# Layer 0 of a conv/attention hybrid: each tile's norm factor and turned y at once, x's last convolution in two blocks, weight products between layer 1's sums

## The chip, the cores and the metric

The kernel runs on one core of a Trainium2 chip. A core has five engines that work side by side and meet at semaphores: PE (TensorE, matrix products into PSUM; its weight loads are listed as PEld), DVE (VectorE), ACT (ScalarE, functions of one input from a table), POOL (GpSimd, which does not read PSUM here) and SP, which starts transfers. Each engine runs its instructions in the order in which they were written to its queue. The metric is the device time of one execution in microseconds (us), as the median of several runs.

## The reference

The input x has 4 images of 256 channels and 32 x 32 pixels (1024 tokens an image, 4096 in all). Four layers follow one another; the change lies in layer 0 and layer 1. Cut to what matters:

```python
# layer 0: a state-space block (Mamba 2), then channel attention
u = layernorm(x as tokens)
z, xBC, dt = split(u @ in_w.T)                 # 256, 256 + 128 + 128, 4 heads
xBC = silu(causal_conv4(xBC) + conv_b)         # per channel, 4 taps along the tokens
x_s, Bm, Cm = split(xBC)
y = scan(dt, A, x_s, Bm, Cm) + Dp * x_s        # recurrence along the tokens of an image
y = y * silu(z)
y = y * rsqrt(mean(y * y, -1) + 1e-5) * rms_w  # norm factor of each token
out = y @ out_w.T
pooled = mean(out, over the image's tokens)
attn = sigmoid(relu(pooled @ se1_w.T + se1_b) @ se2_w.T + se2_b)
x = x + out * attn                             # attn: one number per image and channel
# layer 1: non-local block with one inner channel, batch norm over everything
g, theta, phi = 1x1 convolutions of x to one channel
y = theta * sum(phi * g) / N                   # per image
x = x + batch_norm(w_w * y)                    # needs sums over all 4096 tokens
# layer 2: self-attention, q = u Wq + bq, k = u Wk + bk, then a mixture of experts
# layer 3: another attention, then an LSTM of 1024 steps
```

## The kernel before

All of x stays in SBUF as `rows`, 32 tiles of 128 tokens by 256 channels. In layer 0 an image is `b` (`B` = 4) and a tile within it `c` (`TPI` = 8). `W` is 512 tokens, `BPI` = 2 such blocks an image, `C` = 2 groups of 128 channels.

**`_project`** (L236 on) goes over eight blocks of 512 tokens: transpose, norm, transpose back, and the product with `in_w`. `z` goes through Silu into `zs`; `xBC` lands transposed (channels on partitions) in `xbc[b]`, four groups m of 128 channels: 0 and 1 are x, 2 is B, 3 is C. Three columns of zeros stand ahead of the tokens (`off` = `DCONV` - 1), for the taps. After each second block the finished image is convolved (`convolve`): `_convolution` multiplies one tap on ACT and adds three on DVE (L340), all 1024 tokens at once, and Silu writes the result over the raw values. The last image is not convolved there: `_convolve_last` does it group by group beside the scan of image 0, with Tanh in place of Silu, so that ACT keeps the table that it needs for the scan (silu(a) = a/2 (1 + tanh(a/2)); the taps are halved for that). At the end of the projection `_decays` makes the exponentials of dt for all tiles, which every scan tile needs.

**`_scan`** (L403) does one tile: PE turns x and B (`ptr`), ACT copies them (`xb`), POOL makes `xdt`, `y` and `xw` from them, PE, ACT and DVE make the decay matrix `m_h`, PE the products `py` and `pst`, DVE adds up y and carries the `state` to the next tile. At last DVE multiplies `zs` by y, and ACT squares it and sums the square of each token into a column of `ss` (L462).

**`_attention`** (L492) is run for a whole image once its eight tiles are scanned, for images 0 to 2 after the second tile of the next image (L219), for image 3 at the end. POOL turns eight columns of `ss` into the norm factor `rstd` (L506, and L507 with a power of -0.5). DVE scales the identity by it, once a tile (`diag`, L514). PE multiplies `zs` by that diagonal, which turns y and norms it in one product (L518); ACT copies 512 tokens at a time over the x groups of `xbc`, which the scan needs no more, and sums them on the way (`part`, L522). `pooled` (L527) goes through the two small attention products, and the result scales the output weights (`w_att`). `_out` (L567) multiplies each turned tile by `w_att` and adds to `rows`. For images 0 to 2 these products stand beside the next image's scan; four of image 2 and all of image 3 stand at the end.

**`_query_weights`** (L580) makes Wq Wk^T (`m_qk`) and bq Wk (`b_qk`) for layer 2, at the end of layer 0. **`_layer1`** (L601) has three sums over partitions, each a product with a matrix of ones (`dots`, `sum`, `sum2`), with short DVE and POOL steps between, then a row (`p_row`, L661) that everything after it adds to `rows`.

What sets the order: a planner. The program issues instructions with their tiles; the planner lists them per engine, those written earlier first where several could run, by its own durations, and adds the semaphores. `issue_after(ins)` holds instructions of PE behind another one in the same queue. PSUM has eight banks: in the scan two each for `ptr`, `pst` and `p_o` (turns, attention and `_out`), one each for `pd` and `py`. Each queue then runs strictly in that order.

Of the kernel before, what the change touches and what calls it, by code (L numbers as in the profile page):

```python
# [169 lines left out]
def _layer0_and_1(s):  # L170
# [5 lines left out]
    with ExitStack() as ctx:  # L176
# [22 lines left out]
            dtr=keep.tile([P, NT, NH], F32, name="dtr"),  # L199
            ss=keep.tile([P, NT], F32, name="ss"),  # L200
        )
        for x in v.xbc:
            nc.gpsimd.memset(x[:, :, :off], 0.0)
        with tc.tile_pool(name="conv", bufs=2, side="right") as conv, ExitStack() as body:
# [10 lines left out]
            for b in range(B):  # L215
                for c in range(TPI):
                    _scan(s, v, pools, b, c)
                    if b == 0 and c % 2 == 0:
                        _convolve_last(s, v, pools, conv, c // 2)  # L219
                    if b == 0 and c == TPI - 1:  # L220
                        _out_weights(s, v, pools)
                    if b > 0 and c == 1:
                        held = _attention(s, v, pools, b - 1)
                    if b > 0 and c >= TPI // 2:
                        n = 1 if b == B - 1 else 2
                        for j in range(n * (c - TPI // 2), n * (c - TPI // 2 + 1)):
                            _out(s, v, pools, b - 1, j, held, "p_o")
# [4 lines left out]
            for j in range(TPI):  # L232
                _out(s, v, pools, B - 1, j, last, "ptr")
            _query_weights(s, pools.ps)
        _layer1(s, v)


def _project(s, v, keep, conv):
# [4 lines left out]
    with ExitStack() as ctx:  # L243
# [65 lines left out]
        def convolve(b):  # L309
            for m in range(NXBC):  # L310
                acc = _convolution(s, v, conv, b, m, s.col["conv_w"], s.col["conv_b"])
                nc.scalar.activation(v.xbc[b][:, m, off:], acc, AF.Silu)
# [4 lines left out]
        for i in range(NBLK):  # L317
            if i + 2 < NBLK:
                load(i + 2)
            if i + 1 < NBLK:  # L320
                turn(i + 1)
            project(i)
            if i == NBLK - 1:
                v.decays = _decays(s, keep, pool, ps, v.dtr)
            if i % BPI == BPI - 1 and i + 1 < NBLK:
                convolve(i // BPI)


def _convolution(s, v, conv, b, m, w, bias):

    nc = s.nc
    off = DCONV - 1
    x = v.xbc[b][:, m, :]
    acc = conv.tile([P, L], F32, name="acc")
    tap = w[:, m * DCONV : (m + 1) * DCONV]
    nc.scalar.activation(
        acc, x[:, off:], AF.Identity, bias=bias[:, m : m + 1], scale=tap[:, off:]
    )
    for j in range(off):
        nc.vector.scalar_tensor_tensor(  # L340
            acc, x[:, j : j + L], tap[:, j : j + 1], acc, ALU.mult, ALU.add
        )
    return acc


def _convolve_last(s, v, pools, conv, m):
# [3 lines left out]
    if m == 0:  # L350
# [3 lines left out]
        nc.gpsimd.tensor_scalar_mul(v.half_b, s.col["conv_b"], 0.5)  # L354
    acc = _convolution(s, v, conv, B - 1, m, v.half_w, v.half_b)
    dst = v.xbc[B - 1][:, m, DCONV - 1 :]
    nc.scalar.activation(dst, acc, AF.Tanh)
# [45 lines left out]
def _scan(s, v, pools, b, c):  # L403
# [3 lines left out]
    (a, head), xbc, zs = v.decay, v.xbc[b], v.zs[b]  # L407
    off = DCONV - 1
    if c == 0:
        v.state = pool.tile([P, NH, HD], F32, name="state")  # L410
    state = v.state
    n = b * TPI + c
    t = slice(off + c * P, off + (c + 1) * P)
    bT, cT = xbc[:, 2, t], xbc[:, 3, t]

    ptr = ps.tile([P, 4, P], F32, name="ptr")
    for m in range(3):
        nc.tensor.transpose(ptr[:, m, :], xbc[:, m, t], s.ident)
    nc.tensor.matmul(ptr[:, 3, :], bT, cT, start=True, stop=True)
# [68 lines left out]


def _attention(s, v, pools, b, beside=()):  # L490


# [11 lines left out]

    rstd = pool.tile([P, TPI], F32, name="rstd")
    nc.gpsimd.tensor_scalar(rstd, v.ss[:, bass.ts(b, TPI)], 1.0 / D, EPS, ALU.mult, ALU.add)  # L506
    nc.gpsimd.tensor_tensor(rstd, rstd, s.power, ALU.pow)  # L507
    yT = v.xbc[b][:, :C, DCONV - 1 :]
    part = pool.tile([P, C, BPI], F32, name="part")
    for i in range(BPI):  # L510
        diag = pool.tile([P, TPB, P], F32, name="diag")
        for j in range(TPB):
            n = i * TPB + j
            nc.vector.tensor_scalar_mul(diag[:, j, :], s.ident, rstd[:, n : n + 1])  # L514
        for k in range(C):
            p = small(P, W)
            for j in range(TPB):
                nc.tensor.matmul(  # L518
                    p[:, bass.ts(j, P)], v.zs[b][:, i * TPB + j, bass.ts(k, P)], diag[:, j, :],
                    start=True, stop=True,  # L520
                )
            nc.scalar.activation(  # L522
                yT[:, k, bass.ts(i, W)], p, AF.Identity, accum_out=part[:, k, i : i + 1]
            )

    pooled = pool.tile([P, C], F32, name="pooled")
    nc.vector.tensor_reduce(pooled, part, AX.X, ALU.add)  # L527
    p = small(NSE, 1)
# [35 lines left out]
    nc.scalar.copy(w[:, :, D:], p.rearrange("p (m i) -> p m i", i=3))  # L564
    return yT, w


def _out(s, v, pools, b, j, held, tag):

    nc = s.nc  # L570
    yT, w = held
    n = b * TPI + j
    p = pools.ps.tile([P, W], F32, name="p_y", tag=tag)[:, : D + 3]
    for k in range(C):
        nc.tensor.matmul(p, yT[:, k, bass.ts(j, P)], w[:, k, :], start=k == 0, stop=k == C - 1)
    nc.vector.tensor_add(s.rows[:, n, :], s.rows[:, n, :], p[:, :D])
# [3 lines left out]
def _query_weights(s, ps):  # L580

    nc = s.nc
    wq, wk = (s.w_l2[:, :, j * D : (j + 1) * D] for j in range(2))
    s.m_qk = s.const.tile([P, C, D], F32, name="m_qk")
    s.b_qk = s.const.tile([P, C], F32, name="b_qk")
    for m in range(C):
        p = ps.tile([P, W], F32, name="p_q", tag="p_o")
        for k in range(C):
            nc.tensor.matmul(
                p[:, :D], wq[:, k, bass.ts(m, P)], wk[:, k, :], start=k == 0, stop=k == C - 1  # L590
            )
        nc.scalar.copy(s.m_qk[:, m, :], p[:, :D])
        for k in range(C):
            nc.tensor.matmul(
                p[:, D : D + 1], wk[:, k, bass.ts(m, P)], s.col["bq"][:, k : k + 1],
                start=k == 0, stop=k == C - 1,
            )
        nc.vector.tensor_copy(s.b_qk[:, m : m + 1], p[:, D : D + 1])


def _layer1(s, v):  # L601
# [4 lines left out]
    with ExitStack() as ctx:  # L606
# [3 lines left out]
        def new(name, *shape):  # L610
            return pool.tile([P, *shape], F32, name=name)

        w2, wg = new("w2", C), new("wg", C)
# [14 lines left out]
        dots = ps.tile([P, B], F32, name="dots")  # L628
        nc.tensor.matmul(dots, s.ones, dot, start=True, stop=True)
        y = s.l1_y = s.const.tile([P, NT], F32, name="l1_y")  # L630
# [6 lines left out]
        def total(name, values):  # L637

            p = ps.tile([P, 1], F32, name=name)
            nc.tensor.matmul(p, s.ones, values, start=True, stop=True)  # L640
            mean = new(f"{name}_mean", 1)
# [16 lines left out]
        for k in range(C):  # L658
            diag = new(f"diag{k}", P)
            nc.vector.tensor_scalar_mul(diag, s.ident, scale[:, k : k + 1])  # L660
            nc.tensor.matmul(p[:, bass.ts(k, P)], s.ones, diag, start=True, stop=True)  # L661
        s.l1_row = s.const.tile([P, D], F32, name="l1_row")
# [1309 lines left out]
```

## Time and profile before

| what | us |
|---|---|
| median of 3 runs (lowest, highest) | 3417.93 (3415.67, 3419.51) |
| the profiled execution, device time | 3415.7 |
| its span, first to last instruction | 3413.9 |
| projection, from the start | about 130 |
| scans of images 0, 1, 2, 3 end (last `zs` product) | 185.0, 223.3, 268.9, 310.8 |
| `pooled` of image 3 | 321.8 |
| last `_out` added to `rows` | 336.2 |
| row of layer 1 ready | 345.2 |

A line of the timeline has the start in us, the length in us, the engine, the line of the kernel, the instruction, its output and inputs with their shapes, and how many it stands for; in square brackets the idle time of that engine before it and what ended it. A line of the groups has the busy time, the mean in ns of one, and the idle time before them. The windows give busy time by engine between two points of time. The granted clock is PE's, 1.00 being full. Most matrix products of fp32 are two instructions each.

### The profile page before, as it was taken

The page shows a single profiled execution, that of the slowest core. Times are in us where ns is not written, and L with a number is a line of the kernel's source. Part 1 is how long each engine was busy: PE and PEld are TensorE (multiplying, and loading weights), DVE is VectorE, ACT ScalarE, POOL GpSimd, SP SyncE. Part 2 cuts the span into 40 slices and gives each one's busy share as a digit, 9 for nine tenths or more (in the row PEclk, how much of TensorE's full clock was granted, in tenths as well). Part 3 has the DMA queues.
Part 4 walks back from the last instruction along what each step waited for, and adds up shares of the span by engine and source line. Part 5 has one row for each costly group of instructions (what it writes and reads, how often), then busy time and mean ns, then how long its engine had stood idle before and what let it go on. Part 6 is the DMA issues. An engine that isn't in the chain of part 4 may idle for free.

```text
span 3413.9 us, 143838 instructions
## 1 busy us (share of the span) xinstructions
PE 3103.3 (91%) x63668; PEld 2493.0 (73%) x63668; DVE 1836.3 (54%) x8185; ACT 1093.6 (32%) x4351; POOL 535.0 (16%) x751
## 2 busy tenths in 40 slices
PE   8888899999999989998988988998998998998887
PEld 5476577688888857777777777777777777777776
DVE  6775654651111144565655555565655555655555
ACT  6754222222222222332332332332332332332222
POOL 2342100124444320001001001001001001001000
PEclk9999899999999999999999999999999999999999
DMA  2000011356666620000000000000000000000000
GB/s 78 10 1 1 1 38 38 109 169 197 194 194 216 193 61 2 4 4 10 4 4 10 4 4 10 4 4 10 4 4 10 4 4 10 4 4 8 6 4 10
DMA packets 49221, 140.28 MB, mean 41 GB/s; under 512 B 4944, under 2 KB 38032, under 8 KB 43856
## 3 DMA queue, kind: packets, MB, share of 16 engines
q0 software_dynamic: 18768, 101.03, 9.6%
q1 hardware_dynamic: 27680, 24.45, 2.2%
q8 instruction: 500, 8.19, 1.0%
q10 hardware_dynamic: 2144, 5.55, 0.5%
q14 instruction: 129, 1.06, 0.1%
HBM read 105.78 MB, written 25.22 MB: 38 GB/s over the span
## 4 chain that ended last, share of the span: by engine, by line
PE 42%; DVE 21%; ACT 11%; issue 5%; ACTq 0%; DMA 0%; POOL 0%; DVEq 0%; SPq 0%; POOLq 0%
PE pre L1797 16%; DVE col L1808 11%; PE ph L1292 7%; PE po L1301 7%; PE pre L1741 6%; ACT tri L1811 5%; DVE scan L1820 5%; DVE hs L1831 4%; PE p_a L1695 3%; PE p_d L1397 1%; PE p_k L1365 1%; PE p_x L1266 0%; ACTq L1811 0%; PE p_w L856 0%; DMA acc<-y,late_rows 0%
## 5 line engine op out<-in xcount | busy, mean ns | idle before, releaser
L1797 PE MATMUL pre<-w_v,hs 128*4 128x64 f32 x49104 | 873.5, 219 | 208.0 <-DVE hs L1831 197.3
L1797 PEld LDWEIGHTS pre<-w_v,hs 128*4 128x4 f32 x49104 | 684.8, 86 | 396.6 <-DVE hs L1831 393.6
L1741 PE MATMUL pre<-xg,pick 128*128 128x64 f32 x6144 | 903.3, 283 | 0.6 <-DVE xg L1708 0.6
L1741 PEld LDWEIGHTS pre<-xg,pick 128*128 128x128 f32 x6144 | 762.9, 191 | 118.2 <-DVE xg L1708 0.9
L1808 DVE STREAM_TRANSPOSE col<-pre 128x64 f32<-128x64 f32 x2048 | 484.5, 250 | 303.9 <-PE pre L1797 289.3
L1811 ACT ACTIVATE tri<-col 128x16 f32<-128x16 f32 x1024 | 229.5, 224 | 1175.4 <-DVE col L1808 1175.4
L1820 DVE TENSOR_TENSOR_SCAN scan<-tri 128x24 f32<-128x24 f32 x1024 | 216.2, 211 | 360.7 <-ACT tri L1811 360.7
L1703 POOL TENSOR_TENSOR xg<-xg,gate_bias 128x192 f32<-128x192 f32 x127 | 74.9, 590 | 1597.9 <-ACT xg L1702 1597.9
L1292 PE MATMUL ph<-xT,wt 128*128 128x256 f32 (+1 forms) x1184 | 253.8, 370 | 2.2 <-ACT hT L1295 1.3
L1295 ACT ACTIVATE hT<-ph,wt 128x256 f32<-128x256 f32 (+1 forms) x296 | 136.6, 462 | 353.1 <-PE ph L1292 343.8
L1301 PE MATMUL po<-wt,hT 128*128 128x256 f32 x1120 | 249.1, 379 | 0.0
L1292 PEld LDWEIGHTS ph<-xT,wt 128*128 128x128 f32 x1184 | 205.7, 189 | 42.8 <-ACT hT L1295 7.4
L1301 PEld LDWEIGHTS po<-wt,hT 128*128 128x128 f32 x1120 | 209.8, 190 | 27.0
L1829 DVE STREAM_TRANSPOSE gate<-row 128x64 f32<-128x64 f32 x1024 | 228.1, 223 | 1.0
L1818 ACT ACTIVATE row<-pre 128x64 f32<-128x64 f32 x1024 | 210.2, 205 | 0.9
L1836 DVE SCALAR_TENSOR_TENSOR tri<-hs,scan 128x8 f32<-128x8 f32 x1023 | 181.5, 177 | 36.1 <-DVE hs L1831 1.5
L1270 DVE COPY xT<-p_x 128x512 f32<-128x512 f32 (+1 forms) x37 | 24.5, 662 | 205.1 <-PE p_x L1266 205.0
L1312 DVE TENSOR_TENSOR y<-po,wt 128x256 f32<-128x256 f32 x70 | 29.6, 424 | 185.8 <-PE po L1301 185.8
L1695 PE MATMUL p_a<-w_u,u 128*32 128x192 f32 x1792 | 119.3, 338 | 0.0
L822 PE MATMUL p_s<-u,q 128*128 128x512 f32 x256 | 117.0, 597 | 0.0
L856 PE MATMUL p_w<-v,prT 128*128 128x256 f32 x512 | 116.0, 379 | 0.7 <-ACT prT L848 0.7
L856 PEld LDWEIGHTS p_w<-v,prT 128*128 128x128 f32 x512 | 95.5, 190 | 15.5 <-issue 2.9
(2474 smaller groups left out, 3277.3 us busy)
## 6 DMA issues: line engine op xcount, KB each, us to landing
xn<-xn SPq DMA_DIRECT2D x8, 516.0 KB, 3.5
x<-in_x_dram SPq DMA_DIRECT2D x16, 256.0 KB, 3.2
acc<-rows SPq DMA_DIRECT2D x8, 512.0 KB, 2.9
out_dram<-part SPq DMA_DIRECT2D x64, 64.0 KB, 1.7
xn_early<-xn SPq DMA_DIRECT2D x6, 516.0 KB, 5.1
rows<-acc SPq DMA_DIRECT2D x6, 512.0 KB, 8.6
w_l<-in_w_l_dram ACTq DMA_DIRECT2D x1, 1092.0 KB, 9.6
rows<-acc SPq DMA_DIRECT2D x4, 256.0 KB, 4.5
```

The costliest lines, as they stand in the source:

```text
L856: nc.tensor.matmul(p, prT[:, n, :], images[g // TPI].v[:, n, :], start=n == 0, stop=n == TPI - 1)
L1292: nc.tensor.matmul(ph, w1[:, k, bass.ts(m, P)], xT[:, k, :], start=k == 0, stop=k == C - 1)
L1301: nc.tensor.matmul(po, hT[:, m, bass.ts(j, P)], w2[:, m, :], start=m == 0, stop=m == NHC - 1)
L1695: nc.tensor.matmul(p[32 * j : 32 * (j + 1), :], u3[i * SG // P][:, k, bass.ts(i % (P // SG), 32)], w_u[:, k, j * Q : (j + 1) * Q], start=k ...
L1741: nc.tensor.matmul(p, pick[:, r].rearrange("p j r -> p (j r)"), xg[i][:, v], start=True, stop=t == 0,)
L1797: nc.tensor.matmul(p[32 * j : 32 * j + B, :], hs[:, t - 1, k * B : (k + 1) * B], w_v[:, k, j * Q + v.start : j * Q + v.stop], start=False, ...
L1808: nc.vector.transpose(col[:, g * C : (g + 1) * C, :].rearrange("p n r -> p (n r)"), pre[t % 2][g])
L1811: nc.scalar.activation(z[:, 2:50].rearrange("p (g q) -> p g q", g=2)[:, :, ::3].rearrange("p g (k b) -> p (g k) b", k=C), col[:, :, :B], A ...
L1818: nc.scalar.activation(row, pre[t % 2][2], AF.Tanh)
L1820: nc.vector.tensor_tensor_scan(scan, z[:, 0 : 3 * S], z[:, 26 : 26 + 3 * S], 0.0, ALU.mult, ALU.add)
L1829: nc.vector.transpose(gate.rearrange("p n r -> p (n r)"), row)
L1836: nc.vector.scalar_tensor_tensor(tri[(t + 1) % 2][:, 28:52:3], h, 0.5, cell, ALU.mult, ALU.mult)
```

## The change

Four things are done differently.

1. The norm factor, the diagonal, the turn and the copy of y are made for each tile right behind its scan (`_by_channel`), not for the image. The factor is made in place in the tile's column of `ss`. Each tile's copy is two ACT instructions of 128 columns, whose sums go into `part`, now one column a tile.
2. The x groups (m = 0, 1) of the last image are convolved in two blocks of 512 tokens: the first in `_project` behind block 6, with Silu, its result written from column 0 on (three columns ahead of its old place, so that the raw values that the second block's taps need stay); the second beside image 0's scan as before. `_tokens` gives the columns of a tile's tokens.
3. `_query_weights` is handed out in pieces: the first matrix behind the first sum of layer 1, the second behind the third, the biases behind the products of the row; each has PSUM banks of its own.
4. `_attention` begins at `pooled`.

```diff
             for b in range(B):
                 for c in range(TPI):
                     _scan(s, v, pools, b, c)
+                    _by_channel(s, v, pools, b, c)
...
                 _out(s, v, pools, B - 1, j, last, "ptr")
-            _query_weights(s, pools.ps)
         _layer1(s, v)
...
             if i % BPI == BPI - 1 and i + 1 < NBLK:
                 convolve(i // BPI)
+            if i == NBLK - BPI:
+                for m in range(C):
+                    acc = _convolution(
+                        s, v, conv, B - 1, m, slice(0, W), s.col["conv_w"], s.col["conv_b"]
+                    )
+                    nc.scalar.activation(v.xbc[B - 1][:, m, :W], acc, AF.Silu)
+
+def _tokens(b, lo, hi):
+    off = 0 if b == B - 1 and hi <= W else DCONV - 1
+    return slice(off + lo, off + hi)
...
-    acc = _convolution(s, v, conv, B - 1, m, v.half_w, v.half_b)
-    dst = v.xbc[B - 1][:, m, DCONV - 1 :]
+    lo = W if m < C else 0
+    acc = _convolution(s, v, conv, B - 1, m, slice(lo, L), v.half_w, v.half_b)
+    dst = v.xbc[B - 1][:, m, DCONV - 1 + lo :]
...
+def _by_channel(s, v, pools, b, c):
+    nc, pool = s.nc, pools.out
+    n = b * TPI + c
+    rstd = v.ss[:, n : n + 1]
+    nc.gpsimd.tensor_scalar(rstd, rstd, 1.0 / D, EPS, ALU.mult, ALU.add)
+    nc.gpsimd.tensor_tensor(rstd, rstd, s.power[:, :1], ALU.pow)
+    diag = pool.tile([P, P], F32, name="diag")
+    nc.vector.tensor_scalar_mul(diag, s.ident, rstd)
+    p = pools.ps.tile([P, W], F32, name="p_o")[:, :D]
+    for k in range(C):
+        nc.tensor.matmul(
+            p[:, bass.ts(k, P)], v.zs[b][:, c, bass.ts(k, P)], diag, start=True, stop=True
+        )
+    for k in range(C):
+        nc.scalar.activation(
+            v.xbc[b][:, k, _tokens(b, c * P, (c + 1) * P)], p[:, bass.ts(k, P)], AF.Identity,
+            accum_out=v.part[:, b, k, c : c + 1],
+        )
...
 def _attention(s, v, pools, b, beside=()):
-    rstd = pool.tile([P, TPI], F32, name="rstd")
-    nc.gpsimd.tensor_scalar(rstd, v.ss[:, bass.ts(b, TPI)], 1.0 / D, EPS, ALU.mult, ALU.add)
-    nc.gpsimd.tensor_tensor(rstd, rstd, s.power, ALU.pow)
-    yT = v.xbc[b][:, :C, DCONV - 1 :]
...
-                yT[:, k, bass.ts(i, W)], p, AF.Identity, accum_out=part[:, k, i : i + 1]
...
-    nc.vector.tensor_reduce(pooled, part, AX.X, ALU.add)
+    nc.vector.tensor_reduce(pooled, v.part[:, b], AX.X, ALU.add)
...
 def _query_weights(s, ps):
-    for m in range(C):
-        p = ps.tile([P, W], F32, name="p_q", tag="p_o")
+    def matrix(m):
+        p = ps.tile([P, D], F32, name=f"p_q{m}")
...
+    return [[lambda: matrix(0)], [], [lambda: matrix(1)]], bias
...
+        beside, bias = _query_weights(s, ps)
+        def summed(dst, values):
+            mm = nc.tensor.matmul(dst, s.ones, values, start=True, stop=True)
+            with tc.issue_after(mm.ins):
+                for f in beside.pop(0):
+                    f()
...
-            nc.tensor.matmul(p[:, bass.ts(k, P)], s.ones, diag, start=True, stop=True)
+            mm = nc.tensor.matmul(p[:, bass.ts(k, P)], s.ones, diag, start=True, stop=True)
+        with tc.issue_after(mm.ins):
+            bias()
```

## The prediction

> **What bounds the kernel now.** I read the engine totals first, then the chain of waits, then busy time by stage, then the order of instructions where two stages meet.
>
> ```profile
> PE 3103.3 (91%) x63668; PEld 2493.0 (73%) x63668; DVE 1836.3 (54%) x8185; ACT 1093.6 (32%) x4351; POOL 535.0 (16%) x751
> ```
>
> The totals are an average over four layers, and the chain of waits followed back from the end shows no piece before 680 us. So layer 0 (the first 337 us) is read from its own stages. All later work needs the row that layer 1 ends with at 345 us, so I pass a microsecond gained before that to the end one for one. PE busy by stage (the columns are start:end, length, then busy time and count of PE, PEld, DVE, ACT and POOL, then the granted clock, DMA share and GB/s):
>
> ```profile
> 132.00:184.00 52.00, 38.15 (x168) 24.34 (x169) 47.60 (x80) 36.07 (x92) 26.91 (x30) 0.90 0.04 14
> 184.00:226.00 42.00, 38.12 (x229) 30.38 (x228) 32.06 (x79) 23.65 (x80) 17.04 (x25) 1.00 0.00 1
> 226.00:268.00 42.00, 38.01 (x218) 30.60 (x217) 30.29 (x77) 22.54 (x75) 15.21 (x22) 0.96 0.00 1
> 268.00:312.00 44.00, 37.16 (x215) 29.37 (x213) 30.91 (x82) 23.37 (x74) 17.32 (x27) 0.96 0.00 1
> 312.00:322.00 10.00, 6.48 (x33) 6.32 (x33) 2.00 (x10) 2.75 (x8) 2.00 (x4) 0.66 0.00 0
> 322.00:337.00 15.00, 14.96 (x73) 11.90 (x74) 6.42 (x17) 2.99 (x16) 0.00 (x0) 1.00 0.00 1
> ```
>
> The scan of image 0 (132 to 184) is held by DVE, 92% busy; the other three by PE, 85 to 91% busy; 312 to 322 by nothing but a chain; 322 to 337 by PE. Where image 1 ends and image 2 begins, the timeline reads:
>
> ```profile
> 224.20 0.57 ACT L433 ACTIVATE m_h<-pd 128x512 f32<-128x512 f32 x1
> 225.49 0.20 POOL L506 TENSOR_SCALAR rstd<-ss 128x8 f32<-128x8 f32 x1
> 225.77 1.64 POOL L507 TENSOR_TENSOR rstd<-rstd,power 128x8 f32<-128x8 f32 x1
> 227.44 1.20 DVE L514 TENSOR_SCALAR diag<-ident,rstd 128x128 f32<-128x128 f32 x2 [3.54 <-POOL rstd L507]
> 228.56 1.11 DVE L434 TENSOR_TENSOR m_h<-m_h,gm 128x512 f32<-128x512 f32 x1
> 229.82 1.08 PE L440 MATMUL py<-xdt,m_h 128*128 128x64 f32 x8 [2.80 <-DVE m_h L434]
> ```
>
> DVE runs in the order written, and the two diagonals stand ahead of `m_h`, which could have started at 224.8. PE idles 2.80 us behind it. The start of image 3 (271 to 275) shows the same 3.54 and 2.80 us. After the last tile:
>
> ```profile
> 311.61 0.19 ACT L462 ACTIVATION_READ_ACCUMULATOR sq<-zs 128x1 f32 x1
> 311.88 0.20 POOL L506 TENSOR_SCALAR rstd<-ss 128x8 f32<-128x8 f32 x1 [5.11 <-ACT sq L462]
> 312.45 1.64 POOL L507 TENSOR_TENSOR rstd<-rstd,power 128x8 f32<-128x8 f32 x1
> 314.12 1.66 DVE L514 TENSOR_SCALAR diag<-ident,rstd 128x128 f32<-128x128 f32 x8 [1.94 <-POOL rstd L507]
> 314.55 6.45 PE L518 MATMUL p_o<-diag,zs 128*128 128x128 f32 x32 [4.81 <-DVE diag L514]
> 321.04 0.60 ACT L522 ACTIVATE xbc<-p_o 128x512 f32<-128x512 f32 x1 [0.30 <-PE p_o L518]
> 321.76 0.16 DVE L527 TENSOR_REDUCE pooled<-part 128x2 f32<-128x4 f32 x1 [5.99 <-ACT xbc L522]
> ```
>
> Ten microseconds pass between the last square and `pooled`, for work on eight tiles of which seven were ready long before. The prices of the one-column forms that the change uses are in layer 3's rows:
>
> ```profile
> L1660 POOL TENSOR_TENSOR rstd<-rstd,power 128x1 f32<-128x1 f32 x28 | 15.9, 569 | 2.3
> L1675 ACT COPY u<-p_a 128x128 f32<-128x128 f32 x56 | 14.9, 265 | 3.7
> L1659 POOL TENSOR_SCALAR rstd<-mv 128x1 f32<-128x1 f32 x28 | 6.0, 216 | 198.0 <-DVE mv L1657 198.0
> ```
>
> **(a) The end of the last image.** Left for the last tile: POOL 0.22 + 0.57, one diagonal (0.28, the median of L514), four matmul instructions (two products, 0.55), two evictions of 0.27 with their accumulator reads of 0.19 (some 0.75 as a pair), and about 0.25 of hand-overs as those in the fence: 2.6 us. From 311.8 that puts `pooled` at 314.4 in place of 321.76: 7.3 us less. Not all is kept. PE ran its last scan product to 309.75, the granted clock fell to 0.50 at 313.6 and came back at 320.0 (stage by stage in steps of 1 us); so the turn itself paid the slow 6.4 us. Now the attention products and the `_out` products inherit a slow spell, and that stage is PE-bound (14.96 of 15). At half clock 5.5 us of it cost 2.7. Bounds: 0 (the clock holds, because the gap is shorter) and 5 (two spells). Taken: -7.3 + 2.7 = **-4.6**. The Trainium skill (TensorE: Matmul & The Clock Gate, What's actually happening) says the clock halves after an idle window of about 3.4 us and is whole again after as long a busy one; the trace has 3.9 and 6.4 us here. By that page the new gap (309.75 to about 313.1) might just escape and this term would be -7.3.
>
> **(b) The starts of images 1, 2 and 3.** The batch-wide factor goes, and with it the DVE stalls of 1.17, 3.54 and 3.54 us. PE, the engine nearest to its limit, loses 2.80 us at each of the two later starts, then runs slow: the clock is 0.93 over 225 to 250 and over 275 to 300, which is 3.5 us at half speed, 1.75 lost each. 2 x (2.8 + 1.75) + 1.2 = **-10.3**. Bounds: from the last `zs` product (L460) of image 0 to that of image 1 it is 38.3 us, from there to that of image 2 45.6, so up to 2 x 7.3 = 14.6; and 0 if the restart of a scan is slow for its own reasons. I take the middle, since PE's own rows give it.
>
> **(c) What every tile now pays.** The work of (b) is not gone but dealt out. Per tile POOL gains 0.78 us (32 x 0.78 = 25, in place of 4 x 1.9), ACT 0.75 in place of 0.39 (four evictions of 0.59 + 0.20 for eight tiles), DVE and PE nothing. ACT has room (24 of 42 us; 36 of 52 in image 0, where the dearer evictions make it about 40). POOL's pair stands in one queue with `xdt`, `y` and `xw` of a later tile, and the diagonal stands on DVE ahead of other work, with PE's products behind it. Bounds: 0 (POOL idled 77 us in 21 waits for `xb`, so much of it fits; no gain, since all that goes is in (b)) and 25 (each lands on the path). Where POOL already decides: PE's weight loads waited for `xw` nine times in 32 tiles (five for the state product, four for `py`). Each of those is later by 0.78: **+7.0**, nearer to the lower end, since most tiles show POOL with time to spare. The smaller PSUM traffic shares the two `p_o` buffers with `_out`; waits of that kind cost 0.24 in three places, and I add none.
>
> A page speaks against this term: the Trainium skill (SBUF - State Buffer, Who interferes with whom) says that a VectorE instruction with two SBUF inputs and a GpSimd one lock each other out for their whole length. The trace agrees: POOL's `y` takes 0.61 us alone and 1.59 beside a 1.27 us convolution tap at 151.5. By that page each of the 16 short POOL instructions of image 0 could wait out one such instruction, which would put up to 16 us more on POOL there and take the gain of (d) and more.
>
> **(d) Image 3's x in two blocks: the scan side.** DVE's row for a tap over 1024 columns is 1.28 us; over 512, by the 128x512 row (L434, 0.68), 0.67. Two of the four channel groups shrink by 3 x 0.61 + 0.55 = 2.4 each: 4.8 off DVE where it is 92% busy. Image 0's eight diagonals (8 x 0.28 = 2.2) come into this stage from the next. Net **-2.6**; bounds -4.8 and 0. ACT loses 2 x (0.6 + 0.5), hidden.
>
> **(e) The projection side.** The same halves now follow block 6: DVE 2 x 3 x 0.67 = 4.0, ACT 2 x (0.64 + 0.55) = 2.4, by halves of its 1.23 and 1.06 rows. DVE between 118 and 121.4 waits 3.9 us in four gaps, and is free again until 124, so almost all is covered; at most one tap is ahead of the last `dtr`, which starts the decays: 0.67. Without that cover it costs 4.0. ACT's Silu may fall behind the Exp of the decays, a table load (1.28) and 0.55 more on the way; I take half. **+1.6**, bounds 0 and 4.3 (two loads, two Silus, a tap).
>
> **(f) Layer 1.** Two of the `p_q` instructions stood in the PE-bound `_out` stage (0.43); the copy of `m_qk` stood ahead of the last `of_y` on ACT (0.25); `dots` waited till 338.91 for the `b_qk` copy to free its bank, though `dot` was there at 338.4 (0.47). Against that, the first matrix (four instructions of 0.215) now stands ahead of the next sum: 0.35, or 1.2 at half clock. The second fits in PE's 1.89 us before the row, the biases in the 4.4 us after it, the copies on an idle ACT. **-0.8**, bounds -1.2 and +0.5.
>
> Sum: -4.6 - 10.3 + 7.0 - 2.6 + 1.6 - 0.8 = -9.7. The profiled execution took 3415.7 us (span 3413.9 and 1.8 around it), which is 2.2 below the median of 3417.9. 3415.7 - 9.7 + 2.2 = **3408**.
>
> **Rivals.** *Every tile stalls as the starts did.* Had the 225 us start had one column, the factor would have come at 225.41 + 0.22 + 0.57 + 0.19 = 226.4, still 1.6 after `m_h` was ready. If DVE waits 0.9 on average in 32 tiles, (c) is 29 and the sum +12: **3430**, slower. It costs more than the rest gains (9.7 + 7.0 = 16.7) from 0.52 us a tile. For it: DVE's order at three starts counted on an earlier factor. Against: DVE idles some 1.3 us a tile in images 1 to 3 already.
>
> *The restart is slow by itself.* The new state, fresh `xb` and the empty pipeline may cost those 5 us, and (b) is 0: +0.6, **3418**, no change. For it: POOL's burst of `xdt`, `y`, `xw` before `rstd` would be there anyway. Against: image 1's start, where DVE waited only 1.17, shows no such hole.
>
> *POOL hides all and the clock holds.* (a) -7.3, (c) 0: -19.4, and with 14.6 for (b) -23.7: **3394 to 3398**. For it: POOL is 36 to 41% busy in images 1 to 3. Against: the nine waits on `xw`.
>
> **How the numbers follow.** Chances: the forecast 0.50 (own range 3400 to 3416), stalls in every tile 0.19, slow restart 0.17, all hidden 0.14. About 0.2% (6.8 us) is what a measurement tells from no change, so faster means under 3411.1: 0.38 of the forecast, all of the last case, 0.02 of the restart, 0.54. Slower, over 3424.8: 0.18 of the stalls and 0.03 of the restart, 0.21. Between: 0.25. 3396 to 3426 leaves out half of the last case (0.07) and two thirds of the stalls (0.13).
>
> **What would show it.** Right: `pooled` of the last image about 2.6 us after its last square; no 3.5 us DVE wait on POOL near 225 or 271; twelve taps of 512 columns, six of them before 124 us; PE's wait for `dots` gone. Wrong: DVE idle before the new diagonals summing to far more than the 10.2 us of now, or PE idle behind them; a third Silu table load; a slow clock over the last `_out` for longer than 6 us.

## The result and the profile after

The changed kernel takes 3428.7 us (median of 7 runs, 3423.9 to 3430.5) against 3417.9 before: the ratio is 1.0029, 95% interval 1.0019 to 1.0039. It is slower by 0.3%. The forecast was 3408; the rival "every tile stalls as the starts did" had said 3430.

The profiled execution of the changed kernel took 3426.2 us, span 3424.5, which is 10.6 more than the span before. The engine totals hardly show it:

```profile
PE 3112.0 (91%) x63668; PEld 2496.5 (73%) x63668; DVE 1836.5 (54%) x8189; ACT 1104.2 (32%) x4452; POOL 551.3 (16%) x807
```

The row of layer 1 is copied out at 354.81 in place of 344.76, 10.05 later (this is the start of the copy; the table before gives its end, 345.2). First the kernel before, then the changed one:

```profile
344.76 0.42 DVE L663 COPY l_row<-p_row 128x256 f32<-128x256 f32 x1 [1.12 <-PE p_row L661]
354.81 0.42 DVE L704 COPY l_row<-p_row 128x256 f32<-128x256 f32 x1 [1.12 <-PE p_row L700]
```

From there on the two executions run in step: the same instructions of layers 2 and 3 are between 7.4 and 10.7 us later up to 1500 us. So the difference is made before 355 us. (The difference of the two rows is used below as a second yardstick. It is free of what later layers add by chance, but it is read from one execution of each kernel, and the chance of that execution's clock in layer 0 is in it.)

The waits between 130 and 340 us (total, times, longest, in us), two lines of the kernel before and two of the changed one:

```profile
DVE diag L514 <- POOL rstd L507: 10.2, 4, 3.5
PE p_o L518 <- DVE diag L514: 4.8, 1, 4.8
DVE diag L519 <- POOL ss L517: 33.3, 29, 2.6
PE p_o L522 <- DVE diag L519: 24.9, 28, 2.4
```

Before, DVE waited 10.2 us in four places for the factor. Now 29 of 32 diagonals wait, 1.15 us on average (1.04 over all 32), and 28 of the 32 turns on PE wait behind them. One of these stalls, in the scan of image 2 (the timeline: start, length, engine, line, output and inputs; in brackets the idle time before):

```profile
237.41 0.19 ACT L483 ACTIVATION_READ_ACCUMULATOR sq<-zs 128x1 f32 x1
...
237.84 0.61 POOL L464 TENSOR_TENSOR y<-xb,rows 128x256 f32<-128x256 f32 x1
...
238.54 0.19 POOL L516 TENSOR_SCALAR ss<-ss 128x1 f32<-128x1 f32 x1
238.81 0.61 POOL L467 TENSOR_TENSOR xw<-xb,tail 128x256 f32<-128x256 f32 x1
239.38 0.55 POOL L517 TENSOR_TENSOR ss<-ss,power 128x1 f32<-128x1 f32 x1
239.97 0.29 DVE L519 TENSOR_SCALAR diag<-ident,ss 128x128 f32<-128x128 f32 x1 [2.45 <-POOL ss L517]
240.17 0.42 DVE L472 TENSOR_TENSOR y_in<-pst,head 128x256 f32<-128x256 f32 x1
...
240.40 0.68 PE L522 MATMUL p_o<-diag,zs 128*128 128x128 f32 x4 [2.10 <-DVE diag L519]
240.51 0.68 DVE L455 TENSOR_TENSOR m_h<-m_h,gm 128x512 f32<-128x512 f32 x1
```

The squares of this tile are summed at 237.60. The factor is ready at 239.93, because the next tile's `xdt` and `y` stand ahead of its first POOL step and `xw` between the two. DVE's queue has the diagonal at its head all that time: it stands idle for 2.45 us, and with it `y_in` and `m_h` of the next tile, which do not need the factor, and PE's whole queue behind the turn.

Busy time by stage after (start:end, length, PE, PEld, DVE, ACT, POOL busy with counts, granted clock, DMA share, GB/s):

```profile
132.00:184.00 52.00, 41.33 (x170) 27.99 (x169) 38.51 (x74) 33.97 (x105) 27.22 (x39) 0.80 0.04 15
184.00:226.00 42.00, 35.48 (x216) 27.73 (x215) 31.37 (x82) 25.85 (x99) 22.70 (x38) 0.99 0.00 1
226.00:268.00 42.00, 35.60 (x193) 27.46 (x192) 25.72 (x65) 23.14 (x89) 18.03 (x35) 0.92 0.00 1
268.00:312.00 44.00, 36.90 (x203) 28.02 (x203) 27.78 (x75) 23.71 (x94) 19.35 (x36) 0.99 0.00 1
```

In the three later stages less PE work is done in the same time than before (35.5 and 35.6 of 42 us against 38.1 and 38.0, 36.9 of 44 against 37.2), and in the first one the clock fell from 0.90 to 0.80.

**Where the 10 us come from.** The last `zs` products of images 0 to 3 start at 190.36, 229.06, 282.75 and 328.53; before it was 182.37, 223.26, 268.88 and 310.77. (The 185.0 that the table before gives for image 0 was the first tile of image 1; its true end is 182.4.) So the scans end 17.8 later. The time from 132 us to there can be split by windows of 1 us each: what PE stood idle, what it lost to a lower clock (busy time times one minus the granted clock), and the rest, which is PE at full clock.

| 132 us to the last zs | length | PE idle | lost to the clock | rest |
|---|---|---|---|---|
| before | 178 | 26.5 | 8.0 | 143.5 |
| after | 196 | 32.2 | 16.8 | 147.0 |
| difference | +18 | +5.7 | +8.8 | +3.5 |

The larger part of the loss is not the idle time itself but the clock. Of the +8.8, 6.3 fall in image 0; the added idle time falls in images 1 to 3. Of the six slow spells of the changed trace in this stretch, four (from 146.9, 177.6, 259.5 and 310.7) have a PE gap that a diagonal ended at their start or within the 3.5 us before it. The other two do not: the first, from 129.8, lies ahead of the first diagonal and makes 2.3 of the +8.8, and the one from 167.4 follows a wait for `au`, which ACT makes. In the 3.5 us before 310.7 PE stands idle for 0.77 us behind a diagonal, 1.00 behind `state` and 0.66 behind the next diagonal; from 308 to 309 it has 0.16 us of work, and from 311 to 317 the clock is 0.50:

```profile
308.00:309.00 1.00, 0.16 (x2) 0.00 (x0) 1.00 (x4) 0.19 (x1) 0.14 (x1) 1.00 0.00 0
...
311.00:312.00 1.00, 1.00 (x5) 1.00 (x6) 1.00 (x4) 0.00 (x0) 0.00 (x0) 0.50 0.00 0
...
316.00:317.00 1.00, 1.00 (x4) 0.48 (x4) 0.57 (x2) 0.23 (x1) 1.00 (x2) 0.50 0.00 0
```

The end of the last image did what was forecast. After:

```profile
329.85 0.20 ACT L483 ACTIVATION_READ_ACCUMULATOR sq<-zs 128x1 f32 x1
330.13 0.19 POOL L516 TENSOR_SCALAR ss<-ss 128x1 f32<-128x1 f32 x1 [2.29 <-ACT sq L483]
330.40 0.19 POOL L653 TENSOR_TENSOR w<-cols 128x2 f32<-128x2 f32 x1
330.56 0.20 POOL L654 TENSOR_TENSOR wg<-cols 128x2 f32<-128x2 f32 x1
330.70 0.55 POOL L517 TENSOR_TENSOR ss<-ss,power 128x1 f32<-128x1 f32 x1
331.29 0.28 DVE L519 TENSOR_SCALAR diag<-ident,ss 128x128 f32<-128x128 f32 x1 [0.96 <-POOL ss L517]
...
333.10 0.17 DVE L547 TENSOR_REDUCE pooled<-part 128x2 f32<-128x16 f32 x1 [1.36 <-ACT xbc L526]
```

From the last square to `pooled` it is 3.05 us in place of about 10, and from the last `zs` to `pooled` 4.57 in place of 10.99: 6.4 gained. Layer 1, from `all` to the row, takes 6.94 in place of 7.65. The books close: 17.8 - 6.4 - 0.3 (`pooled` to the last `_out`) - 0.3 (to `all`) - 0.7 = 10.1.

### The profile page after: what moved, and what is told of

Its sections match the earlier page's. It is cut to its first block, busy times and chain, and to the rows that moved or that the text cites. A ratio compares the mean times of both kernels' runs of the same rounds, so it can differ in the third digit from the quotient of the medians.

```text
span 3424.5 us, 143950 instructions
## 1 busy us (share of the span) xinstructions
PE 3112.0 (91%) x63668; PEld 2496.5 (73%) x63668; DVE 1836.5 (54%) x8189; ACT 1104.2 (32%) x4452; POOL 551.3 (16%) x807
## 3 DMA queue, kind: packets, MB, share of 16 engines
q14 instruction: 129, 1.06, 0.1%
## 4 chain that ended last, share of the span: by engine, by line
PE 54%; DVE 25%; ACT 11%; issue 6%; POOL 2%; DMA 0%; ACTq 0%; DVEq 0%; SPq 0%; POOLq 0%
PE pre L1838 16%; DVE col L1849 11%; PE ph L1333 7%; PE po L1342 7%; PE pre L1782 6%; ACT tri L1852 5%; DVE scan L1861 5%; DVE hs L1872 4%; PE p_a L1736 3%; PE p_w L897 3%; PE p_s L863 3%; DVE acc L360 1%; PE p_d L1438 1%; PE py L461 1%; PE p_w L884 1%
```

## The experiments

The theory after the result: **diagonal waits**. DVE's queue is strict, the diagonal stands in it where the planner takes the factor to be ready, and the factor comes later; that stalls DVE, then PE, then the clock. Rivals: the **added work** itself (POOL's 25 us, ACT's dearer evictions, the turns' share of the PSUM buffers) delays the tiles and the waits only show it; or the **scan starts cold** (in the changed trace the clock is 0.53 from 130 to 137 us, where it was 1.00 before), so that the two-block convolution is to blame.

The results in one table. Ratios are to the kernel before on the same chip; its medians were 3415.9 beside e1 to e4, 3416.5 beside e5 to e8 and 3421.9 beside e9, e10 and e12, and gains "by the medians" are against these. "Row" is the time of layer 1's row in the one execution that was traced, less the 344.76 of before; for e1, e8 and e12 that execution was the slowest of its kernel. The last four columns are as in the table above.

| run | median | ratio (95%) | row | length | idle | clock | rest |
|---|---|---|---|---|---|---|---|
| after | 3428.7 | 1.0029 (1.0019 to 1.0039) | +10.1 | 196 | 32.2 | 16.8 | 147.0 |
| e1 rest only | 3411.1 | 0.9983 (0.9974 to 0.9992) | -1.6 | 179 | 22.9 | 14.0 | 142.1 |
| e2 tiles only | 3429.7 | 1.0041 (1.0027 to 1.0055) | +15.8 | 200 | 36.4 | 15.7 | 147.9 |
| e3 ready column | 3389.6 | 0.9925 (0.9911 to 0.9938) | -26.1 | 162 | 13.2 | 4.5 | 144.3 |
| e4 a tile later | 3393.9 | 0.9936 (0.9922 to 0.9949) | -17.1 | 169 | 16.3 | 7.2 | 145.5 |
| e5 longer chain | 3432.8 | 1.0045 (1.0031 to 1.0058) | +19.1 | 203 | 38.1 | 17.0 | 147.9 |
| e6 last image | 3413.0 | 0.9987 (0.9978 to 0.9996) | -7.9 | 176 | 23.0 | 7.3 | 145.7 |
| e7 starts held | 3405.8 | 0.9964 (0.9950 to 0.9978) | -11.7 | 166 | 17.2 | 5.7 | 143.0 |
| e8 written later | 3404.4 | 0.9957 (0.9943 to 0.9970) | -8.3 | 173 | 21.3 | 5.9 | 145.8 |
| e9 one step | 3412.7 | 0.9975 (0.9964 to 0.9986) | -4.8 | 182 | 25.3 | 9.9 | 146.7 |
| e10 tiles held | 3407.2 | 0.9957 (0.9943 to 0.9970) | -9.0 | 174 | 18.5 | 11.0 | 144.6 |
| e12 starts and last | 3405.0 | 0.9948 (0.9935 to 0.9962) | -9.6 | 168 | 19.1 | 3.4 | 145.5 |

The column "rest" stays within 142 and 148 in all of them: what the edits move is PE's idle time and its clock.

### Which part loses: e1 and e2

e1 is the changed kernel with part 1 undone:

```diff
                     _scan(s, v, pools, b, c)
-                    _by_channel(s, v, pools, b, c)
...
+    rstd = pool.tile([P, TPI], F32, name="rstd")
+    nc.gpsimd.tensor_scalar(rstd, v.ss[:, bass.ts(b, TPI)], 1.0 / D, EPS, ALU.mult, ALU.add)
+    nc.gpsimd.tensor_tensor(rstd, rstd, s.power, ALU.pow)
```

> The changed kernel with part 1 undone (factor, turn and copy for a whole image in the attention as before; image 3's x in two blocks and the weight products between layer 1's sums stay). Theory 'diagonal waits' (DVE's queue stands at every tile's diagonal until POOL has the factor): the loss of 10.8 us is all in part 1, so this kernel is 3414 to 3418, my terms (d)+(e)+(f) = -1.8 on 3417.9. Rival 'scan starts cold' (the half convolution in the projection makes the scan of image 0 start late and at half clock, +5.4 us at its end): 3421 to 3425, above the kernel before.

e2 is the kernel before with part 1 alone:

```diff
                     _scan(s, v, pools, b, c)
+                    _by_channel(s, v, pools, b, c)
```

> The kernel before with part 1 alone (factor, diagonal, turn and copy at each tile). 'Diagonal waits': at least the whole loss, 3427 to 3433, with about 33 us of DVE waits for the factor in 32 tiles. 'Scan starts cold': 3420 to 3424, because image 0's 5.4 us come from the projection side, and the end of image 0's scan is then near 185 us.

Without part 1 the kernel is faster than before, by 1.6 us at the row (its median, 4.9 below, lies under the range given); with part 1 alone it is slower, by 15.8 at the row, and its median and its waits are where the theory had them. So the loss is part 1's, and the cold start falls as its cause: e1 keeps the two-block convolution and starts as cold (2.6 us lost to the clock between 132 and 140 us, where the kernel before has 2.4 us of idle time instead), it loses 14.0 us to the clock in the scan, nearly as much as the changed kernel, and still is not slower. Nor does the cold start need that convolution: e10, further down, is without it and has a clock of 0.57 from 130 to 137 us. And e2's image 0, without that convolution, ends at 192.97, later than the 190.36 of the changed kernel. e2's waits:

```profile
DVE diag L500 <- POOL ss L498: 34.0, 30, 2.6
PE p_o L503 <- DVE diag L500: 29.6, 28, 2.6
```

### Is it the wait or the work: e3 and e4

e3 scales the diagonal by a column that is ready since the projection. It leaves the norm factor out of layer 0's output; POOL still makes it. All other work is there.

```diff
-    nc.vector.tensor_scalar_mul(diag, s.ident, rstd)
+    nc.vector.tensor_scalar_mul(diag, s.ident, v.tail[:, n, :1])
```

> The changed kernel, but the diagonal is scaled by a column that is ready since the projection, so that no diagonal waits for POOL; POOL still makes all 32 factors, ACT all 64 evictions, PE all turns. The output of layer 0 is therefore not normed by the factor. 'Diagonal waits': the 33 us of DVE waits go and the scans end 15 to 25 us earlier, 3400 to 3412. Rival 'added work' (POOL's 25 us, ACT's dearer evictions, the shared PSUM buffers of the turn are what delays the tiles, and the DVE waits only show it): 3424 to 3430, with the waits moved to PE for zs or to PSUM buffers.

e4 computes the same as the changed kernel. Each tile's factor and turn are written behind the next tile's scan, and the diagonal is held on DVE behind that tile's `zs` product (`_scan` returns it as `done`, and `issue_after` with an instruction of DVE holds the block's DVE instructions behind it):

```diff
-                    _scan(s, v, pools, b, c)
-                    _by_channel(s, v, pools, b, c)
+                    done = _scan(s, v, pools, b, c)
+                    if b + c > 0:
+                        with tc.issue_after(done.ins):
+                            _by_channel(s, v, pools, *divmod(b * TPI + c - 1, TPI))
...
+            _by_channel(s, v, pools, B - 1, TPI - 1)
             beside = [
```

> The changed kernel with each tile's factor and turn written behind the next tile's scan and its diagonal held on DVE behind that tile's zs product; the same work, but about 5 us between a tile's square and its diagonal. 'Diagonal waits': nearly all DVE waits for the factor go, 3400 to 3414; the last tile's turn is not held. 'Added work': 3424 to 3430, because POOL, ACT and PE do all that they did.

Both gain more than the theory had said: the row is 36.1 and 27.1 us earlier than in the changed kernel. (e3's later layers see other data, so for it the row counts.) The added work falls as a cause: e4 has the same 64 POOL instructions, 64 evictions and 128 turn products, and is 22 us faster than the kernel before. Its waits between 130 and 340 us:

```profile
DVE diag L523 <- POOL ss L521: 5.1, 4, 2.4
PE p_o L526 <- DVE diag L523: 2.4, 2, 2.1
```

33.3 us of DVE waits have become 5.1, 24.9 us of PE waits 2.4; PE's idle time in the scan is half of what it was (16.3 against 32.2), and the clock's loss less than half (7.2 against 16.8). In the timeline of e4 a diagonal starts where its engine has just finished something else, with no wait in brackets:

```profile
229.21 0.73 DVE L484 TENSOR_TENSOR zs<-zs,y 128x256 f32<-128x256 f32 x1
229.87 0.63 DVE L523 TENSOR_SCALAR diag<-ident,ss 128x128 f32<-128x128 f32 x1
230.42 0.41 DVE L481 TENSOR_TENSOR state<-state,pst 128x256 f32<-128x256 f32 x1
```

e4 beats both kernels: 3393.9 us, 0.5 to 0.8% below the kernel before.

### The dose: e5, e9 and e8

e5 puts two more small POOL instructions between factor and diagonal:

```diff
     nc.gpsimd.tensor_tensor(rstd, rstd, s.power[:, :1], ALU.pow)
+    nc.gpsimd.tensor_scalar(rstd, rstd, 1.0, 0.0, ALU.mult, ALU.add)
+    nc.gpsimd.tensor_scalar(rstd, rstd, 1.0, 0.0, ALU.mult, ALU.add)
```

> The changed kernel with two more POOL instructions (128x1, times one) between each tile's factor and its diagonal, some 0.4 to 0.5 us more a tile, 32 x 0.45 = 14 us in all. 'Diagonal waits': 29 of the 32 diagonals waited for POOL, so nearly all of it lands on the path unless the planner moves the diagonal: 3436 to 3445. 'POOL has room' (what I took for most tiles in term (c)): 3428 to 3433.

e9 takes away one of the changed kernel's own two POOL steps; it leaves the 1e-5 out of the norm factor, so that its later layers see other data:

```diff
-    nc.scalar.activation(sq, zs[:, c, :], AF.Square, accum_out=v.ss[:, n : n + 1])
+    nc.scalar.activation(sq, zs[:, c, :], AF.Square, scale=D**-0.5, accum_out=v.ss[:, n : n + 1])
...
-    nc.gpsimd.tensor_scalar(rstd, rstd, 1.0 / D, EPS, ALU.mult, ALU.add)
```

> The changed kernel with one POOL instruction per tile between square and diagonal in place of two: ACT's square scales by 1/16, and the 1e-5 in the norm factor is left out. The chain is shorter by 0.27 us a tile, and POOL's xw can no longer come between the two. 'Diagonal waits': the 33 us of DVE waits shrink by 8 to 13 us and the time by half of that or all, 3416 to 3424. 'Planner's order': since the planner may move the diagonal forward by what it believes it gained, no change, 3425 to 3429.

e8 is e4 without the hold: only the place in the program changes.

```diff
-                        with tc.issue_after(done.ins):
-                            _by_channel(s, v, pools, *divmod(b * TPI + c - 1, TPI))
+                        _by_channel(s, v, pools, *divmod(b * TPI + c - 1, TPI))
```

> As the run a tile later, but without the hold: each tile's factor and turn are only written behind the next tile's scan, and the planner may put the diagonal wherever it holds the factor to be ready. 'Diagonal waits by the planner's order': the planner still counts on an early factor, over 10 us of DVE waits for it remain, 3402 to 3425. If the place in the program settles the order: as that run, 3392 to 3397.

DVE's waits for the factor follow the dose. First e5, then e9, then e8:

```profile
DVE diag L521 <- POOL ss L519: 40.5, 29, 3.4
```

```profile
DVE diag L518 <- POOL ss L516: 26.0, 27, 2.1
```

```profile
DVE diag L521 <- POOL ss L519: 17.2, 15, 3.1
```

The sizes missed on both sides. e5 adds some 14 us of POOL work; 7.2 more of DVE waits come of it, and 9.0 at the row; the median rose by only 4 (5.5 by the ratios), below the 8 to 16 that the theory had said and inside what "POOL has room" had. e9 takes 7.3 us of waits away, and the row is 14.8 earlier, the median 16.0 lower, more than the theory had said: 6.9 of it less idle time on PE and 6.9 less lost to the clock. So the link between waits and time is not one for one: a hole in PE can cost a slow spell on top, and which holes do differs from run to run. e8 has half of the waits left: of its 31 diagonals that have a next tile, 30 still stand ahead of that tile's `zs` product in DVE's queue, where in e4 all 31 stand behind it, and 15 diagonals wait. The place in the program moved them back a little; the hold does the rest.

### My two gains by themselves: e6, e7, e12 and e10

e6 gives part 1 to image 3 only, held as in e4; images 0 to 2 as before. It measures term (a).

```diff
+                    if b == B - 1 and c > 0:
+                        with tc.issue_after(done.ins):
+                            _by_channel(s, v, pools, b, c - 1)
```

> The kernel before, with part 1 for image 3 alone, each tile's diagonal held behind the next tile's zs product so that it does not wait; images 0 to 2 as before. It measures term (a). With my sum (-7.3 + 2.7 for a slow clock handed on to the last _out): 4 to 5 us less than before, 3411 to 3414. If the shorter gap keeps the clock whole, as the changed kernel's trace shows: 6 to 8 less, 3408 to 3411. If the seven early tiles cost image 3's scan what they save at its end: no change, 3415 to 3418.

e7 is the kernel before with the attention of images 0 to 2 held behind the next image's second `zs` product. It measures term (b).

```diff
                     if b > 0 and c == 1:
-                        held = _attention(s, v, pools, b - 1)
+                        with tc.issue_after(done.ins):
+                            held = _attention(s, v, pools, b - 1)
```

> The kernel before, with the whole of the attention's DVE work (the eight diagonals first) held behind the zs product of the next image's second tile, so that no scan start waits for the factor; nothing else is changed. It measures term (b). With my sum: the DVE waits of 3.5 us at the starts of images 2 and 3 go, and 8 to 14 us with them: 3403 to 3409. Rival 'the restart is slow by itself': 3414 to 3418.

e12 has both edits, e10 is the kernel before with part 1 held as in e4 (e4 without parts 2 and 3).

> The kernel before with the two earlier edits together: the attention of images 0 to 2 held behind the next image's second tile, and part 1 with held diagonals for image 3 alone. If the two add up: -3.5 - 10.7 = -14, 3400 to 3405; the same as the run with all tiles held, if what part 1 can gain is only (a) and (b). If turning every tile by itself gains more than that, this one is slower than the run with all tiles held by over 5 us.

> The kernel before with part 1 alone, each tile's diagonal held behind the next tile's zs product. If the tiles' pieces cost nothing once no diagonal waits, this gives what (a) and (b) gave alone (-3.5 and -10.7), or a little more: 3399 to 3403. If the pieces still cost the 7 us of my term (c): 3407 to 3411. From the run a tile later (3394) it should differ only by parts 2 and 3, 2 to 5 us.

e7 gives (b) almost to the number: 10.7 us by the medians, 11.7 at the row, where the sum had 10.3; images 1 to 3 take 35.5, 41.5 and 38.3 us in place of 40.9, 45.6 and 41.9. The slow restart falls as a rival: at the starts of images 2 and 3 e7 keeps a PE gap behind `xw` (1.14 and 1.56 us, 1.07 and 1.06 before), and the 2.80 behind `m_h` is gone. Its eight diagonals run in one go, and `m_h` stands ahead of them:

```profile
227.06 1.14 DVE L435 TENSOR_TENSOR m_h<-m_h,gm 128x512 f32<-128x512 f32 x1
...
228.79 0.50 DVE L461 TENSOR_TENSOR zs<-zs,y 128x256 f32<-128x256 f32 x1
229.22 2.38 DVE L516 TENSOR_SCALAR diag<-ident,rstd 128x128 f32<-128x128 f32 x8
```

e6 has `pooled` 4.20 us after the last `zs` (10.99 before), but needs 15.90 from there to the last `_out` (14.45 before): 6.8 - 1.45 = 5.3 gained. At the row it is 7.9, since its image 3 is scanned 1.9 faster too and the images before it, where nothing was changed, end 0.7 earlier. By the medians e6 gains 3.5, inside the range that my sum had given.

By the medians e12's two gains add: it is 17.0 below the kernel before on its chip, where e6 and e7 had 3.5 and 10.7 (as ratios, 0.9948 against 0.9964 for e7, whose intervals overlap). In the traced execution they do not: its row is at 335.13, e7's at 333.11. There the scan of image 3 takes 1.9 longer than in e7, and the 6.5 us that the end gains (`pooled` 4.72 after the last `zs`, e7 11.23) are lost again by a slow spell of about 16 us, where the clock fell behind a PE gap of 1.79 us at 299.8:

```profile
300.00:303.00 3.00, 1.42 (x8) 1.17 (x8) 1.62 (x5) 1.13 (x6) 1.00 (x4) 0.94 0.01 3
303.00:319.00 16.00, 14.84 (x45) 11.53 (x44) 4.03 (x12) 2.18 (x12) 0.11 (x1) 0.50 0.01 1
319.00:327.00 8.00, 8.00 (x35) 6.17 (x34) 3.37 (x8) 1.33 (x8) 0.00 (x0) 0.96 0.00 0
```

e10's median is above the range I gave for free pieces and at the lower end of the one with 7 us of cost; but the kernel before was slower on this chip too (3421.9), and by ratio e10 and e12 are not told apart. So of what part 1 gives in its best form, (a) and (b) are about all. e4 and e10 differ by 8 us at the row: 5.2 at the end of image 0, where part 2's shorter taps lie and e10 had the lower clock (0.83 against 0.89), 0.8 in layer 1, and most of the rest between `pooled` and the last `_out`. How much of the 5.2 is part 2 and how much the clock by chance was not separated.

## Why the prediction was wrong, point by point

- **(a) The end of the last image, -4.6.** The mechanism was right. In the changed kernel it gave -6.7 (-6.4 to `pooled`, -0.3 behind it): the clock stayed at 1.00 from 319 to 348 us, so the +2.7 for a slow spell handed on did not occur there. It is no constant: 1.45 in e6, and in the traced execution of e12 it ate the whole gain. What I left out is that the turns of seven of the eight tiles do not vanish but move into the scan of image 3, where PE is near its limit: 7 x 0.55, some 4 us, about the size of the +3.5 in "rest". One reading was off: the clock fell at about 313.3, not 313.6 (it is 0.63 from 313 to 314, and PE has no work until 314.55), so the trace has some 3.5 and 6.8 us where I had 3.9 and 6.4.
- **(b) The starts, -10.3.** The mechanism is shown by e7 (-10.7, -11.7 at the row): images 2 and 3 gain 4.1 and 3.6, where I had 4.55 each. That the total fits so well is in part luck: image 1 gains 5.4 where I had 1.2, and image 0, where nothing was changed, ends 1.2 later. The upper bound of 14.6 rested on the wrong end of image 0: with 40.9 for image 1 in place of 38.3 it is 2 x 4.7 = 9.4, below the term itself. In the changed kernel this gain was there and was spent: image 1's scan, for one, is 2.2 shorter than before, image 2's 8.1 longer.
- **(c) What every tile pays, +7.0. This step failed.** I counted the work that POOL does more, at the places where PE's weight loads waited for `xw` (nine by my count, eight in the trace: five and three), and took the value near the lower end "since most tiles show POOL with time to spare". POOL's spare time was not what mattered: the price is paid on DVE, whose queue stands still from the diagonal's turn to the factor's arrival, in 29 of 32 tiles. Part 1 alone costs 15.8 at the row (e2) although (a) and (b) in it are worth 7.9 and 11.7 (e6, e7), so (c) is about 35 at the row, or 28 by the medians (13.8 + 3.5 + 10.7); going by e12, which has (a) and (b) together, it is 25 and 31. The rival had it at 29, from 0.9 us of DVE wait a tile; measured were 1.04 over the 32 tiles. The break-even of 0.52 us a tile that I gave was passed in the trace by a factor of two.
- **The evidence that I set against that rival was wrong.** "DVE idles some 1.3 us a tile already" says nothing, since in a strict queue idle time elsewhere is no cover for a wait at the head. The row that spoke for it, DVE standing ahead of `m_h` at three starts, was the measurement of the very same wait, and I had worked out that even a one-column factor would come 1.6 us late there.
- **The clock.** I priced it at the end and at two starts. In the scan it was worth +8.8, more than the idle time itself (+5.7), and 2.3 of it lay ahead of the first diagonal.
- **(d) and (e), -2.6 and +1.6.** About right. e1, which has (d), (e) and (f) alone, gains 1.6 at the row, where the sum had 1.8 (by the medians it is 4.9, more than I had). Image 0's scan from first to last `zs` is 1.4 us shorter in e1 than before, and 2.9 shorter in the changed kernel than in e2. The first `zs` of the scan comes 0.4 later (139.76 against 139.32; 0.8 in e1), not 1.6: there was no third table load for Silu, and the halves lie before the decays. The halves' taps take 0.75 us in the projection and 0.86 in the scan, not 0.67; what that cost was not measured.
- **(f) Layer 1, -0.8.** Right: -0.7. `dots` starts 0.14 us after `dot` ends, where it was 0.55 before.
- **The page on the shared port** (the Trainium skill, SBUF - State Buffer, Who interferes with whom), by which image 0 might pay up to 16 us: e4 has all of image 0's POOL pairs and ends that image at 183.32, 0.95 later than before. The stretch is there: the one-column step takes 0.19 to 1.05 us in e4, the longest two beside a tap of 1.65 us. Its price stays open: e10, without part 2's shorter taps, ends image 0 at 188.53, 6.2 later than before and with a lower clock (0.83 against 0.90), so it is well below 16 us, but no run separates it.

Of the signs that I named, the wrong one appeared as written: DVE idle before the new diagonals (33.3 us) far above 10.2, and PE idle behind them. The right ones appeared as well (`pooled` 3.05 us after the last square, no 3.5 us wait near 225 or 271, the short taps before 124 us, no wait for `dots`): each of them showed that a saving was there, and none could show what the tiles paid for it.

## What to carry to other kernels

Small steps across engines (ACT to POOL to DVE to PE) cost by where the last of them stands in its in-order queue more than by their lengths: here two steps of 0.19 and 0.55 us a tile cost 25 to 35 us in 32 tiles. Ask of each new wait what stands behind it, and multiply by the number of tiles. The remedy is to move the waiting instruction back by one tile of other work, explicitly, since the planner here put it ahead of that work even when it was written behind it (e8). Where PE is near its limit, a gap can be paid twice, once as idle time and once by the clock behind it, so prefer the version with fewer gaps even at equal work.

## What was not expected of the hardware

The clock's answer to a gap is not fixed. At the same place in layer 2 PE stood idle for 1.72 us in the kernel before, and the clock stayed at 1.00; in e1 it stood idle for 1.73 us and then ran at half speed for about 10 us, which put 5.0 us between the two executions. e1:

```profile
681.46 1.64 PE L167 MATMUL p_w<-ident,xn 128*128 128x128 f32 x8 [1.73 <-DVE xn L158]
```

```profile
682.00:694.00 12.00, 12.00 (x39) 7.83 (x39) 5.04 (x23) 1.28 (x3) 0.00 (x0) 0.57 0.13 46
694.00:706.00 12.00, 11.85 (x62) 10.26 (x60) 6.71 (x29) 2.38 (x4) 0.00 (x0) 1.00 0.00 0
```

The kernel before, at the same place:

```profile
683.23 1.65 PE L167 MATMUL p_w<-ident,xn 128*128 128x128 f32 x8 [1.72 <-DVE xn L158]
```

```profile
684.00:696.00 12.00, 12.00 (x69) 9.46 (x69) 7.50 (x33) 3.29 (x7) 0.00 (x0) 1.00 0.13 46
```

This would explain why e1's eleven executions lie between 3406.7 and 3418.1, while e4's five lie within 1.6 us; that such spells make the whole spread was not tested. Seven of the thirteen traces of this case have a spell at this place (e1, e2, e5, e6, e8, e10, e12).

The traces show one thing more. In all thirteen, every spell of half clock that ended within the execution lasts a whole number of stretches of 3.41 us, from one to seven: e1's here is three, e12's of about 16 us is five. Cut into such stretches, up to 720 us, each of the 85 falls of the clock comes behind a stretch in which PE, as the profile shows it, was busy for 73% or less, and each of the 85 returns behind one with 83% or more. But many stretches between 44 and 73% brought no fall, so this busy time alone does not settle it.

The Trainium skill (TensorE: Matmul & The Clock Gate, What's actually happening) has a free-running window of some 3.4 us, which agrees with the whole stretches and with an outcome that differs from run to run. But it puts the fall behind an idle window of that length, and here gaps of under 1.8 us were enough.
